# A graph attention kernel: ScalarE's exponentials ahead of its table copies, own rows transposed a block earlier

## The chip, the cores and the metric

The kernel runs on one NeuronCore of a Trainium2 chip. The metric is the device time of one execution in microseconds (us). A core has five engines with a queue of instructions each: TensorE (PE in the profile; its weight loads are PEld), VectorE (DVE), ScalarE (ACT), GpSimd (POOL) and SyncE (SP). They wait for one another through semaphores. Here GpSimd issues the gathers, SyncE issues most other DMAs.

## The reference

A graph of 6250 nodes with 256 features and 100,000 edges, sorted by destination, goes through three attention layers. The first two are of one kind (4 heads of 64), with a self loop at each node, and an ELU between them; the third has 8 heads of 32. Cut to what matters:

```python
def _gatv2_layer(x, src, dst, n, Wl, Wr, att, b):
    xl = (x @ Wl).reshape(n, H, C)
    xr = (x @ Wr).reshape(n, H, C)
    e = jax.nn.leaky_relu(xl[src] + xr[dst], NEG_SLOPE)
    logits = jnp.einsum('ehc,hc->eh', e, att)
    m = jax.ops.segment_max(logits, dst, num_segments=n)
    ex = jnp.exp(logits - m[dst])
    denom = jax.ops.segment_sum(ex, dst, num_segments=n)
    alpha = ex / (denom[dst] + 1e-16)
    msg = xl[src] * alpha[:, :, None]
    out = jax.ops.segment_sum(msg, dst, num_segments=n)
    return out.reshape(n, H * C) + b
...
h = _gatv2_layer(x, src, dst, n, Wl1, Wr1, att1, b1)
h = jax.nn.elu(h)
h = _gatv2_layer(h, src, dst, n, Wl2, Wr2, att2, b2)
...
x = _layernorm(x + _L0_gnn_ref(...), axis=-1)
x = _layernorm(x + _L1_gnn_ref(x, ...), axis=-1)
```

## The kernel before

The nodes are sorted by their number of edges and cut into 49 blocks of 128 (NB), one node to a partition. A node's neighbours lie along the columns: a block has 39 columns at first and 10 at the end, the node itself among them in the first two layers. The columns are cut into tiles `g` of at most 9 (T), for which nine buffers are kept. GpSimd fills them by one indirect DMA for each column (L1207), out of a table with a row for each node.

`layer2` runs the first two attention layers: layer 0 with `own1`, `finish1` and the table `xl1_d`, layer 1 with `own2`, `finish2` and the table `xl2_d`. The third layer follows in the last part of `tile_by_degree` and isn't touched. The text counts blocks from 0 in each layer.

There is no scheduler: each engine's instructions stand in the order in which the program calls them, and each engine takes its own in that order. So what counts is the order of calls in the loop over blocks b of `layer2`:

- `gather(b + 1)` issues the gathers of the next block. `ready(b + 1)` calls `own`, which makes the next block's own rows. In layer 0, `own1` transposes the block's features on TensorE, copies them to SBUF on ScalarE (`transposed`, L1256) and multiplies them by two matrices (`product`, L1261): `pl`, for column 0 of `g`, and `pr`, which stays in PSUM. In layer 1, `own2` takes both from a tile `two` that SyncE has loaded: a copy of `pr` to PSUM (L1516).
- `attend(b)`: on VectorE for each tile a maximum, a multiplication and a sum (L1396 to L1398) give the logits. `weights` takes their maximum over the columns (L1272), then ScalarE makes four exponentials, one for each head, with their sums (L1279), and copies the weights of the last few columns (`by`, L1286). After that `later` copies the next block's own row to column 0 (L1477 in layer 0, L1517 in layer 1). In layer 0 ScalarE also keeps the sorted positions (L1408).
- `end(b - 1)`: VectorE divides the finished sum of the block before by its denominators (L1415) and adds the bias. In layer 0 `finish1` makes the ELU: three activations on ScalarE (L1481, L1482, L1484), and on VectorE the sum of their results (L1489). In layer 1 `finish2` adds the input (L1520) and makes the layer norm: statistics on VectorE, two small activations on ScalarE (L1350, L1351), a small instruction on VectorE (L1355) and the norm on ScalarE (L1358).
- The reciprocal of the block's denominators (L1447) on VectorE.
- `weighted_sum(b)`: VectorE multiplies each tile by its weights (L1309), ScalarE does so for the last few columns, one head of one column at a time (L1308), and TensorE adds the columns up by matmuls with the identity into `acc` (L1316). After the first tile's multiplication `between` is called: it runs the function `rest` of `finish`, with L1489 or L1355. So these stand on VectorE between the first and the second multiplication.
- Then the function `last` of `finish` writes the output rows of block b - 1, which are the next layer's tables: transposes on TensorE, their copy on ScalarE (L1256), products, and copies of these (twice L1496 in layer 0; L1531 and L1532 in layer 1), and SyncE stores them.

PSUM holds two buffers each of `pr` and the weights `wt`, two of the tag "tp", which the transposes and products share, one of `acc`.

At block 47 `follow` issues the first gathers of the next layer, for its first three blocks, from rows of blocks 0 to 44 alone.

Of the kernel before, what the change touches and what calls it, by code (L numbers as in the profile page):

```python
# [26 lines left out]
F32 = mybir.dt.float32  # L27
# [8 lines left out]
P = 128  # L36
# [1092 lines left out]
def tile_by_degree(  # L1129
# [3 lines left out]
    nc = tc.nc  # L1133
# [3 lines left out]
    NB = -(-N // P)  # L1137
# [3 lines left out]
    W2 = H2 * (D2 + 1)  # L1141
# [8 lines left out]
    def per_head(t, H):  # L1150
        return t.rearrange("p (h d) -> p h d", h=H)
# [6 lines left out]
    x1 = near[:, :, CM:]  # L1158
# [43 lines left out]
    def gather_rows(b, rows, cut, own, table, of, width, j0, j1):  # L1202


        for g, (s0, s1) in zip(rows, cut):
            for j in range(max(s0 - own, j0), min(s1 - own, j1)):
                nc.gpsimd.indirect_dma_start(  # L1207
                    out=g[:, j + own - s0, :width], out_offset=None, in_=table,
                    in_offset=source(of, b, j),
                )  # L1210

    def row_tiles(b, own):
        cut = chunks(cols[b] + own)
        return [rowp.tile([P, T, RW], F32, name="g") for _ in cut], cut
# [33 lines left out]
            nc.vector.reduce_sum(bad, pb, axis=AX.X)  # L1248
            nc.vector.tensor_single_scalar(done, bad, 0.0, op=OP.is_equal)

    def transposed(work, ps, xt):
        pt = ps.tile([P, 2, P], F32, name="pt", tag="tp")
        for c in range(2):
            nc.tensor.transpose(pt[:, c, :], xt[:, c * P : (c + 1) * P], ident)
        xT = work.tile([P, 2, P], F32, name="xT")
        nc.scalar.copy(xT, pt)  # L1256
        return xT

    def product(pm, xT, w):
        for c in range(2):  # L1260
            nc.tensor.matmul(pm, xT[:, c, :], w[:, c, :], start=c == 0, stop=c == 1)  # L1261
# [6 lines left out]
    def weights(work, ps, lg, S, H, scalar=0):  # L1268


        top = work.tile([P, H], F32, name="top")
        nc.vector.tensor_reduce(  # L1272
            top, lg[:, :S, :].rearrange("p s h -> p h s"), axis=AX.X, op=OP.max, negate=True
        )
        wt = ps.tile([P, S, H], F32, name="wt")
        den = work.tile([P, H], F32, name="den")
        if H <= 4:
            for h in range(H):
                nc.scalar.activation(  # L1279
                    wt[:, :, h], lg[:, :S, h], AF.Exp, bias=top[:, h : h + 1],  # L1280
                    accum_out=den[:, h : h + 1],
                )
            by = None
            if scalar:
                by = work.tile([P, scalar, H], F32, name="by")
                nc.scalar.copy(by, wt[:, S - scalar :, :])  # L1286
            return (wt, by), lambda: den
        nc.vector.tensor_add(lg[:, :S, :], lg[:, :S, :], top[:, None, :].to_broadcast([P, S, H]))
        nc.scalar.activation(wt, lg[:, :S, :], AF.Exp)  # L1289

        def add_up():
            nc.vector.reduce_sum(den, wt.rearrange("p s h -> p h s"), axis=AX.X)
            return den

        return (wt, None), add_up
# [64 lines left out]
    def layer2(i, table, of, width, start, own, finish, follow):  # L1360

        with ExitStack() as es:
            zp = es.enter_context(tc.tile_pool(name=f"z{i}", bufs=1))
            work = es.enter_context(tc.tile_pool(name=f"work{i}", bufs=3))
            ps = es.enter_context(tc.tile_pool(name=f"ps{i}", bufs=2, space=PSUM))
            ps1 = es.enter_context(tc.tile_pool(name=f"ps1{i}", bufs=1, space=PSUM))  # L1370
            pst = es.enter_context(tc.tile_pool(name=f"pst{i}", bufs=2, space=PSUM))
            at = ps1.tile([P, W2], F32, name="at")
            nc.scalar.copy(at, att[i])
            state = {}

            def gather(b):
                first = EARLY[b] if b in begun else 0
                rows, cut = begun.pop(b) if first else row_tiles(b, 1)
                gather_rows(b, rows, cut, 1, table, of, width, first, cols[b])
                state[b] = [rows, cut]  # L1380

            later = []

            def ready(b):
                pr, put = own(work, ps, pst, b, state[b][0][0][:, 0, :W2])
                state[b].append(pr)
                later.append(put)

            def attend(b):
                rows, cut, xr = state.pop(b)  # L1390
                S = cols[b] + 1
                lg = work.tile([P, CM + 1, H2], F32, name="lg")
                for g, (s0, s1) in zip(rows, cut):
                    n = s1 - s0
                    z = zp.tile([P, T, W2], F32, name="z")[:, :n, :]
                    nc.vector.tensor_max(z, g[:, :n, :W2], xr[:, None, :].to_broadcast([P, n, W2]))  # L1396
                    nc.vector.tensor_mul(z, z, at[:, None, :].to_broadcast([P, n, W2]))  # L1397
                    nc.vector.reduce_sum(  # L1398
                        lg[:, s0:s1, :], z.rearrange("p t (h d) -> p t h d", h=H2), axis=AX.X
                    )  # L1400
                few = min(S // 3, cut[-1][1] - cut[-1][0] - 1) if b + 1 < NB else 0
                wt, new = weights(work, ps, lg, S, H2, few)
                while later:
                    later.pop()()
                if i == 0:
                    for g, (s0, s1) in zip(rows, cut):
                        s = max(s0, 1)
                        nc.scalar.copy(spots[:, b, s - 1 : s1 - 1], g[:, s - s0 : s1 - s0, W2])  # L1408
                    if 0 < b <= len(EARLY):
                        sort_sources(work, pst, b - 1)  # L1410
                return rows, cut, wt, new

            def end(b, acc, den):
                h = work.tile([P, F], F32, name="h")
                nc.vector.tensor_mul(  # L1415
                    per_head(h, H2), per_head(acc, H2),
                    den.unsqueeze(2).to_broadcast([P, H2, D2]),
                )
                if i == 0:
                    nc.vector.tensor_add(h, h, bias[0])  # L1420
                return finish(work, pst, b, h)

            for b in range(3):
                if (i, b) not in loaded:
                    start(b)
            gather(0)
            ready(0)
            later.pop()()
            if i == 0:
                none(state[0][2])  # L1430
            acc, den, rest = None, None, None
            for b in range(NB):
                if b + 3 < NB:
                    start(b + 3)
                if b + 1 < NB:
                    gather(b + 1)
                if b + 2 == NB:
                    follow()
                if b + 1 < NB:
                    ready(b + 1)  # L1440
                rows, cut, wt, new = attend(b)
                if b:
                    rest = end(b - 1, acc, den)
                if i == 0:
                    nc.vector.tensor_add(x1[:, b, :], x1[:, b, :], bias[1])
                den = new()
                nc.vector.reciprocal(den, den)  # L1447

                last = []

                def between():
                    if b:
                        last.append(rest())

                acc = weighted_sum(ps1, rows, cut, wt, H2, D2 + 1, between)
                if i == 0 and b + 1 < NB:
                    none(state[b + 1][2])
                if last:
                    last[0]()
            end(NB - 1, acc, den)()()  # L1460

    def none(t):
# [5 lines left out]
            out=near[:, b, :], out_offset=None, in_=near_d[:, :], in_offset=node(b)  # L1468
        )

    def own1(work, ps, pst, b, row):
        xT = transposed(work, pst, x1[:, b, :])
        pl = pst.tile([P, W2], F32, name="pl", tag="tp")
        product(pl, xT, wc[0][:, 0])
        pr = ps.tile([P, W2], F32, name="pr")
        product(pr, xT, wc[0][:, 1])
        return pr, lambda: nc.scalar.copy(row, pl)  # L1477

    def finish1(work, pst, b, h):
        neg = work.tile([P, F], F32, name="neg")  # L1480
# [29 lines left out]
        nc.sync.dma_start(two[:, 1, :], xr2_d[b * P : (b + 1) * P])  # L1510
        kept[b] = two

    def own2(work, ps, pst, b, row):
        two = kept.pop(b)
        pr = ps.tile([P, W2], F32, name="pr")
        nc.scalar.copy(pr, two[:, 1, :])  # L1516
        return pr, lambda: nc.scalar.copy(row, two[:, 0, :])  # L1517

    def finish2(work, pst, b, h):
        nc.vector.tensor_add(h, h, x1[:, b, :])  # L1520
# [18 lines left out]
    kept, loaded = {}, set()  # L1539
# [11 lines left out]
    with ExitStack() as es:  # L1551
        work = es.enter_context(tc.tile_pool(name="work3", bufs=3))
        ps = es.enter_context(tc.tile_pool(name="ps3", bufs=3, space=PSUM))
        state = {}
# [50 lines left out]
        acc, den, puts, rest = None, None, {}, None  # L1605
        for b in range(NB):
# [5 lines left out]
            if b:  # L1612
                rest = end(b - 1, acc, den)
# [39 lines left out]
```

## Time and profile before

| What | us |
|---|---|
| median of 3 runs | 3907.3 (3907.01 to 3914.32) |
| profiled execution | 3906.24 |
| its span, first to last instruction | 3904.4 |
| VectorE busy | 2859.7 (73%) |
| GpSimd busy | 2558.8 (66%) |
| TensorE matmuls busy | 1465.1 (38%) |
| ScalarE busy | 1093.2 (28%) |

Layer 0 lasts from about 220 to 1440 us of the span, layer 1 from about 1540 to 2720, the third layer from there to the end; what comes before 220 us sorts the nodes and builds the first table. A row of a group of instructions tells line, engine, operation, the tiles written and read with their sizes, the count, then busy time in us and the mean of one in ns, then the idle time of the engine just before them and what ended most of it. "remote" there is a releaser that the trace doesn't tell. A row of a timeline has the start and duration in us, engine, line, operation, tiles, count, and in brackets the idle time before it. A row of windows has for each engine its busy time and number of instructions, then the granted TensorE clock, the DMA share and GB/s.

### The profile page before, as it was taken

How to read it: one execution, taken by the hardware profiler on the slowest of the kernel's cores; microseconds unless marked ns; L12 is line 12 of the kernel's file. 1: busy time of each engine (PE TensorE's matmuls, PEld its weight loads, DVE VectorE, ACT ScalarE, POOL GpSimd, SP SyncE). 2: the span in 40 equal slices, each digit the busy share in tenths (PEclk: the TensorE clock that was granted, in tenths of full speed). 3: DMA queues.
4: the chain of work that ended last, by engine and by line, in shares of the span. 5: the costliest groups of instructions: out<-in, count | busy, mean ns of one | idle time of the engine just before them, and what ended most of it. 6: DMA issues, size and time to landing. Idle time of an engine off the chain costs nothing.

```text
span 3904.4 us, 23669 instructions
## 1 busy us (share of the span) xinstructions
PE 1465.1 (38%) x5147; PEld 1100.0 (28%) x5147; DVE 2859.7 (73%) x2624; ACT 1093.2 (28%) x4179; POOL 2558.8 (66%) x2642
## 2 busy tenths in 40 slices
PE   5335655646667653355545455554000000000000
PEld 4223443435455542243433334442000000000000
DVE  6267888768888867798877889895686666666655
ACT  2123433434445441243334334442000000000000
POOL 6466666666666654666666666663777777777774
PEclk8667787777888886676766777776555555555555
DMA  8443333333334333333434344342433333333332
GB/s 192 101 94 100 104 103 100 105 102 103 105 103 107 104 102 71 103 106 105 112 104 111 107 110 111 109 111 69 100 107 105 97 96 97 97 97 96 97 97 56
DMA packets 197563, 399.62 MB, mean 102 GB/s; under 512 B 63516, under 2 KB 115994, under 8 KB 197396
## 3 DMA queue, kind: packets, MB, share of 16 engines
q0 software_dynamic: 123488, 342.06, 33.7%
q1 hardware_dynamic: 66226, 54.22, 4.9%
q10 hardware_dynamic: 7698, 1.74, 0.4%
q8 instruction: 45, 0.74, 0.1%
q14 instruction: 106, 0.87, 0.1%
HBM read 357.84 MB, written 40.42 MB: 102 GB/s over the span
## 4 chain that ended last, share of the span: by engine, by line
issue 24%; POOL 21%; PE 16%; DVE 14%; another core or an unknown queue 12%; ACT 9%; DMA 2%; DVEq 0%; SPq 0%; ACTq 0%; POOLq 0%
POOL g L1207 19%; PE acc L1316 10%; ACT g L1308 4%; PE pm L1261 3%; DVE z L1397 3%; DVE z L1396 3%; DVE lg L1398 3%; ACT wt L1279 2%; DVE weighted L1327 1%; DVE g L1309 1%; DMA g<-xl_d,near_r 1%; POOL out L1597 1%; ACT xT L1256 1%; PE pl L1261 1%
## 5 line engine op out<-in xcount | busy, mean ns | idle before, releaser
L1207 POOL DMA_INDIRECT g<-xl_d,near_r x1591 | 1508.6, 948 | 843.6 <-issue 455.7
L1316 PE MATMUL acc<-g,ident 128*128 128x256 f32 x3452 | 1015.0, 455 | 910.1 <-issue 361.4
L1316 PEld LDWEIGHTS acc<-g,ident 128*128 128x128 f32 x3452 | 768.0, 229 | 1152.9 <-issue 617.4
L1207 POOL DMA_INDIRECT g<-whs_d,near_r x777 | 802.2, 1032 | 293.9 <-issue 251.9
L1308 ACT ACTIVATE g<-g,by 128x64 f32<-128x64 f32 x2064 | 550.4, 337 | 331.3 <-issue 328.0
L1396 DVE TENSOR_TENSOR z<-g,pr 128x1820 f32<-128x1820 f32 (+4 forms) x236 | 503.4, 2133 | 39.3 <-DMA g<-xl_d,near_r 25.7
L1397 DVE TENSOR_TENSOR z<-z,at 128x1820 f32<-128x1820 f32 (+4 forms) x236 | 503.7, 2134 | 8.1
L1398 DVE TENSOR_REDUCE lg<-z 128x28 f32<-128x1820 f32 (+4 forms) x236 | 503.6, 2134 | 8.1
L1336 DVE TENSOR_REDUCE acc_v<-weighted 128x256 f32<-128x4096 f32 (+16 forms) x49 | 349.2, 7127 | 11.7 <-remote 6.1
L1309 DVE TENSOR_TENSOR g<-g,wt 128x1792 f32<-128x1792 f32 (+5 forms) x236 | 353.8, 1516 | 2.9
L1567 DVE TENSOR_TENSOR lg<-g,s_r 128x56 f32<-128x56 f32 (+4 forms) x113 | 22.8, 214 | 367.4 <-DMA g<-whs_d,near_r 300.0
L1289 ACT ACTIVATE wt<-lg 128x128 f32<-128x128 f32 (+17 forms) x49 | 14.0, 285 | 901.2 <-DVE top L1272 309.9
L1256 ACT COPY xT<-pt 128x256 f32<-128x256 f32 x147 | 55.0, 374 | 704.8 <-remote 367.3
L1327 DVE TENSOR_TENSOR weighted<-g,wt 128x1792 f32<-128x1792 f32 (+4 forms) x113 | 229.5, 2048 | 0.0
L1447 DVE RECIPROCAL den<-den 128x4 f32<-128x4 f32 x98 | 17.4, 177 | 226.8 <-ACT wt L1279 158.9
L1279 ACT ACTIVATE wt<-lg,top 128x19 f32<-128x19 f32 (+14 forms) x392 | 116.1, 296 | 209.0 <-DVE top L1272 83.7
L1415 DVE TENSOR_TENSOR h<-acc,den 128x256 f32<-128x256 f32 x98 | 40.7, 416 | 166.8 <-remote 122.3
L1261 PE MATMUL pm<-wh_cat,xT 128*128 128x272 f32 x196 | 83.9, 568 | 192.7 <-issue 108.7
L1261 PE MATMUL pm<-wcat,xT 128*128 128x260 f32 x392 | 138.5, 512 | 45.8 <-ACT xT L1256 44.8
L1261 PEld LDWEIGHTS pm<-wcat,xT 128*128 128x128 f32 x392 | 96.9, 261 | 82.1 <-ACT xT L1256 61.7
L1261 PEld LDWEIGHTS pm<-wh_cat,xT 128*128 128x128 f32 x196 | 46.0, 260 | 213.5 <-issue 113.5
L1597 POOL DMA_INDIRECT out<-y,node_i x49 | 50.3, 1027 | 49.6 <-ACT y L1358 35.6
(180 smaller groups left out, 1511.1 us busy)
## 6 DMA issues: line engine op xcount, KB each, us to landing
g<-xl_d,near_r POOLq DMA_INDIRECT x1591
g<-whs_d,near_r POOLq DMA_INDIRECT x777
whs_d<-row SPq DMA_DIRECT2D x49, 132.0 KB
xl_d<-xl SPq DMA_DIRECT2D x49, 130.0 KB
xl_d<-row SPq DMA_DIRECT2D x49, 130.0 KB
xr_d<-row SPq DMA_DIRECT2D x49, 130.0 KB
two<-xl_d SPq DMA_DIRECT2D x49, 130.0 KB
two<-xr_d SPq DMA_DIRECT2D x49, 130.0 KB
```

The lines of the kernel that those rows point to most:

```text
L1207: nc.gpsimd.indirect_dma_start(out=g[:, j + own - s0, :width], out_offset=None, in_=table, in_offset=source(of, b, j),)
L1256: nc.scalar.copy(xT, pt)
L1261: nc.tensor.matmul(pm, xT[:, c, :], w[:, c, :], start=c == 0, stop=c == 1)
L1279: nc.scalar.activation(wt[:, :, h], lg[:, :S, h], AF.Exp, bias=top[:, h : h + 1], accum_out=den[:, h : h + 1],)
L1308: nc.scalar.mul(g4[:, t, h, :], g4[:, t, h, :], by[:, t - m, h : h + 1])
L1309: nc.vector.tensor_mul(g4[:, :m], g4[:, :m], wt[:, s0 : s0 + m, :].unsqueeze(3).to_broadcast([P, m, H, F // H]),)
L1316: nc.tensor.matmul(acc, ident, g4[:, t], start=s0 + t == 0, stop=s0 + t == S - 1)
L1327: nc.vector.tensor_mul(prod[:, s0 - base : s1 - base, :].rearrange("p t (h d) -> p t h d", h=H), g[:, :n, :F].rearrange("p t (h d) -> p t ...
L1336: nc.vector.reduce_sum(part, prod[:, : s1 - base, :].rearrange("p s f -> p f s"), axis=AX.X)
L1396: nc.vector.tensor_max(z, g[:, :n, :W2], xr[:, None, :].to_broadcast([P, n, W2]))
L1397: nc.vector.tensor_mul(z, z, at[:, None, :].to_broadcast([P, n, W2]))
L1398: nc.vector.reduce_sum(lg[:, s0:s1, :], z.rearrange("p t (h d) -> p t h d", h=H2), axis=AX.X)
```

## The change

In `layer2` three calls move. `own` is cut in two: its first half (the transposes and their copy, in layer 0 alone) runs two blocks ahead, after `end(b - 1)` and the reciprocal, and gives back a function for the products. `ready(b + 1)`, which calls that function and the copy to column 0, moves from ahead of `attend(b)` into it, to just after the exponentials. `last(b - 1)` moves from the end of iteration b to iteration b + 1, after its exponentials and after `ready`. In `own1` the product `pr` is made ahead of `pl`, and the transposed tile has a name, and so three buffers, of its own.

So ScalarE's order in a block of layer 0 was: table copies of block b - 2 (L1256, twice L1496), copy of the own transposes for b + 1 (L1256), exponentials of b (L1279, L1286), L1477, L1408, the ELU of b - 1 (L1481 to L1484), multiplications of b (L1308). It becomes: exponentials of b, L1477 for b + 1, table copies of b - 2, L1408, the ELU of b - 1, copy of the own transposes for b + 2, multiplications of b. In layer 1 the copies L1516 and L1517 follow the exponentials, then the table copies (L1256, L1531, L1532), then L1350, L1351, L1358 and the multiplications. TensorE's order was sum of b - 1, transposes and products of the output b - 2, own transposes and products for b + 1; it becomes sum of b - 1, own products for b + 1, transposes and products of the output b - 2, own transposes for b + 2. VectorE, GpSimd and SyncE keep their orders.

```diff
-    def transposed(work, ps, xt):
+    def transposed(work, ps, xt, name="xT"):
...
-        xT = work.tile([P, 2, P], F32, name="xT")
+        xT = work.tile([P, 2, P], F32, name=name)
...
-            later = []
+            mine, due = {}, []
 
             def ready(b):
-                pr, put = own(work, ps, pst, b, state[b][0][0][:, 0, :W2])
+                pr, put = mine.pop(b)(state[b][0][0][:, 0, :W2])
                 state[b].append(pr)
-                later.append(put)
+                put()
...
                 wt, new = weights(work, ps, lg, S, H2, few)
-                while later:
-                    later.pop()()
+                if b + 1 < NB:
+                    ready(b + 1)
+                while due:
+                    due.pop()()
...
             gather(0)
+            for b in range(2):
+                mine[b] = own(work, ps, pst, b)
             ready(0)
-            later.pop()()
...
-                if b + 1 < NB:
-                    ready(b + 1)
                 rows, cut, wt, new = attend(b)
...
-                last = []
+                if b + 2 < NB:
+                    mine[b + 2] = own(work, ps, pst, b + 2)
 
                 def between():
                     if b:
-                        last.append(rest())
+                        due.append(rest())
 
                 acc = weighted_sum(ps1, rows, cut, wt, H2, D2 + 1, between)
                 if i == 0 and b + 1 < NB:
                     none(state[b + 1][2])
-                if last:
-                    last[0]()
+            due.pop()()
             end(NB - 1, acc, den)()()
...
-    def own1(work, ps, pst, b, row):
-        xT = transposed(work, pst, x1[:, b, :])
-        pl = pst.tile([P, W2], F32, name="pl", tag="tp")
-        product(pl, xT, wc[0][:, 0])
-        pr = ps.tile([P, W2], F32, name="pr")
-        product(pr, xT, wc[0][:, 1])
-        return pr, lambda: nc.scalar.copy(row, pl)
+    def own1(work, ps, pst, b):
+        xT = transposed(work, pst, x1[:, b, :], "xo")
+
+        def products(row):
+            pr = ps.tile([P, W2], F32, name="pr")
+            product(pr, xT, wc[0][:, 1])
+            pl = pst.tile([P, W2], F32, name="pl", tag="tp")
+            product(pl, xT, wc[0][:, 0])
+            return pr, lambda: nc.scalar.copy(row, pl)
+
+        return products
...
-    def own2(work, ps, pst, b, row):
-        two = kept.pop(b)
-        pr = ps.tile([P, W2], F32, name="pr")
-        nc.scalar.copy(pr, two[:, 1, :])
-        return pr, lambda: nc.scalar.copy(row, two[:, 0, :])
+    def own2(work, ps, pst, b):
+        def products(row):
+            two = kept.pop(b)
+            pr = ps.tile([P, W2], F32, name="pr")
+            nc.scalar.copy(pr, two[:, 1, :])
+            return pr, lambda: nc.scalar.copy(row, two[:, 0, :])
+
+        return products
```

## The prediction

> **What bounds the kernel now.** I read the page first (shares of the engines, the chain), then the busy time by stage, then the groups of VectorE in each stage with the idle time before them, and last the timeline of one block of each layer. VectorE (DVE) is the busiest engine, 73%, and in the two attention layers it is at four fifths and more:
>
> ```profile
> core 0: us, PE busy (x) PEld busy (x) DVE busy (x) ACT busy (x) POOL busy (x), PEclk, DMA share, GB/s
> 220.00:1440.00 1220.00, 751.39 (x2608) 553.17 (x2608) 983.41 (x883) 509.57 (x1920) 786.15 (x828) 0.79 0.38 102
> 1600.00:2670.00 1070.00, 556.97 (x1882) 425.92 (x1882) 934.49 (x760) 436.29 (x1776) 686.34 (x725) 0.72 0.40 107
> ```
>
> The first row is layer 0 of the two (47 blocks), the second layer 1. GpSimd (POOL), which issues the gathers, has a third of each stage left. So what VectorE waits for sets the pace. In layer 0 and in layer 1 its groups with idle time before them are these:
>
> ```profile
> L1447 DVE RECIPROCAL den<-den 128x4 f32<-128x4 f32 x47 | 8.3, 178 | 132.5 <-ACT wt L1279 88.7 <-issue 43.8
> L1415 DVE TENSOR_TENSOR h<-acc,den 128x256 f32<-128x256 f32 x47 | 19.5, 415 | 61.4 <-PE acc L1316 33.6 <-remote 27.8
> ...
> L1447 DVE RECIPROCAL den<-den 128x4 f32<-128x4 f32 x47 | 8.3, 177 | 76.0 <-ACT wt L1279 64.3 <-issue 11.7
> L1415 DVE TENSOR_TENSOR h<-acc,den 128x256 f32<-128x256 f32 x46 | 19.1, 415 | 42.2 <-remote 42.2
> ```
>
> The reciprocal waits for ScalarE's exponentials. Why they are late, a block of layer 0 tells (ScalarE's rows, then VectorE's):
>
> ```profile
> 1062.35 0.37 ACT L1256 COPY xT<-pt 128x256 f32<-128x256 f32 x1 [7.69 <-PE pt L1254]
> 1064.91 0.38 ACT L1496 COPY row<-pm 128x260 f32<-128x260 f32 x1 [2.19 <-PE pm L1261]
> 1066.14 0.37 ACT L1496 COPY row<-pm 128x256 f32<-128x256 f32 x1 [0.85 <-PE pm L1261]
> 1066.41 0.38 ACT L1256 COPY xT<-pt 128x256 f32<-128x256 f32 x1
> 1066.67 0.31 ACT L1279 ACTIVATE wt<-lg,top 128x16 f32<-128x16 f32 x1
> ...
> 1068.54 0.38 ACT L1477 COPY g<-pl 128x260 f32<-128x260 f32 x1
> 1068.81 0.41 ACT L1408 CAST near_r<-g 128x7 int32<-128x7 f32 x2
> 1069.13 0.41 ACT L1481 ACTIVATE neg<-h 128x256 f32<-128x256 f32 x1
> ...
> 1069.89 0.40 ACT L1484 ACTIVATE pos<-h 128x256 f32<-128x256 f32 x1
> ...
> 1062.88 0.26 DVE L1272 TENSOR_REDUCE top<-lg 128x4 f32<-128x64 f32 x1
> ...
> 1068.47 0.18 DVE L1447 RECIPROCAL den<-den 128x4 f32<-128x4 f32 x1 [4.20 <-ACT wt L1279]
> 1068.68 2.29 DVE L1309 TENSOR_TENSOR g<-g,wt 128x2048 f32<-128x2048 f32 x1
> 1070.89 0.42 DVE L1489 SCALAR_TENSOR_TENSOR h<-neg,pos 128x256 f32<-128x256 f32 x1
> ...
> 1071.23 0.95 DVE L1309 TENSOR_TENSOR g<-g,wt 128x768 f32<-128x768 f32 x1
> ```
>
> The maximum was there at 1063.14, the exponentials began at 1066.67: 3.5 us of row copies and their waits for TensorE stood ahead of them. And see the place of L1489: between the two multiplications L1309, in order, and it reads what ScalarE's L1484 writes. Today L1484 is done before the first multiplication ends, so L1489 costs no wait.
>
> **What the Trainium skill says.** "TensorE: Matmul & The Clock Gate", section "Architectural detail": ScalarE and VectorE take their instructions in strict order. The trace agrees: no row of theirs overtakes another. Same page, "HAM oscillation": TensorE falls to half clock after idle gaps of about 3.4 us; the granted clock here is 0.79 and 0.72 in the two layers, and 0.50 in the last stage, where no matmul runs. "Perfetto Trace Analysis", section "Per-engine timelines": a matmul's end in a trace is computed, not observed. That fits the waits called remote: VectorE sat 27.8 us (twice) and 42.2 us (seven times) before L1415, though the last sum shows long ended.
>
> **The change part by part.**
>
> *Gain: exponentials first.* They now follow ScalarE's multiplications of the block before, and wait for the maximum alone. What idle time stays before the reciprocal: the four of them take 1.8 us from the maximum to the reciprocal, VectorE's own work there lasts 1.13 us in layer 0 (1063.14 to 1064.27), and 1.46 us in layer 1 (one addition and the two statistics more, 2272.73 to 2274.19). So 0.69 and 0.35 us stay. 132.5 - 47 x 0.69 = 100 us and 76.0 - 47 x 0.35 = 60 us go: 160 us in all.
>
> *Cost in layer 0: L1489 becomes a wait.* ScalarE's order after the exponentials is now: the small copy, the own row's copy L1477, then the copies for the next table (L1256, twice L1496), and only then casts and L1481 to L1484. From the end of the last exponential (1068.31 in the block above): the copy L1256 at +0.55, if its transposes are ready; the first L1496 2.17 us later (mean of the 49 blocks, 1.61 to 2.57, as it waits for two matmuls); the second 1.11 us later (0.88 to 1.73, one of 7.31 left out); the casts 0.27 later; the end of L1484 1.54 after them. Sum: 5.64 us. VectorE's L1489 is due at 1070.89, that is at +2.58. So VectorE stands for 3.06 us in every block, with the second multiplication and all the next block's work queued behind it: 47 x 3.06 = 144 us. Nothing hides this: VectorE is the pacing engine.
>
> *Cost in layer 1: L1355 becomes a wait.* It also stands between two multiplications and reads L1351. After the exponentials (end 2274.89) now come the copies L1516 and L1517, then L1256 at +0.88, L1531 2.23 later (mean; 1.64 to 2.64 and two outliers), L1532 +0.27, L1350 +0.06, the end of L1351 +0.52: 3.96 us. L1355 was at 2277.46, +2.57. That is 1.39 us, 47 times, less 10 us for the seven blocks where VectorE waits for the sum longer anyway: 55 us.
>
> *Products behind the sum.* TensorE's queue is now sum, own products, output's transposes. The own products are in the timeline as two rows of 1.15 and 1.04 us, 2.2 us together, and the output's transposes as 0.63 us. Where ScalarE's multiplications run nearly to the maximum (blocks 7 to 14 of layer 0; in block 10 from 573.08 to a last sum at 593.22), L1477 and L1256 wait for these 1 to 2.5 us more: 15 us. In other blocks these are done before the exponentials end, at no cost. The sum's start moves from +2.6 to about +5, as the next table's matmuls stand ahead of it; the sum has 20 us until L1415 asks for it, so nothing, and up to 85 us if that cover is gone (rival below).
>
> *Rows a block ahead, buffers.* Transposes of own rows are as many as before, their copy (0.38 us) leaves the way of the exponentials and stands ahead of ScalarE's multiplications: nothing. The new tile has three buffers and is used one block later. Row tiles too: nothing.
>
> *DMAs.* The two stores of a block's output rows come 7 us later on SP. Only GpSimd's first gather for layer 1 waits for one of them (1418.10, for a store issued at 1415.55), and after those early gathers GpSimd stands still for 23.9 us until 1493.93 for the last rows. 7 us lie within it. Gathers and stores are the same in number and order: nothing. The same at the end of layer 1.
>
> Sum: -160 + 144 + 55 + 15 = +54 us. The profiled execution took 3906.2 us (span 3904.4), the median is 3907.3, 1 us above. Forecast 3960 us.
>
> **Rivals.**
>
> *The waits are short and the gain stays (faster).* If TensorE is at full clock when the two copies wait, they cost 1.61 + 0.88 and 1.65 us: waits of 2.27 and 0.81 us, 107 and 38 us in all. If half of the 70 us of remote waits before L1415 goes too, the sum is -160 + 107 + 38 - 35 = -50: 3857 us. For it: the clock depends on how TensorE's idle time is cut, and that is what is changed; the short values are the commonest single ones. Against: the means hold long values for half of the blocks.
>
> *ScalarE or TensorE sets the pace (much slower).* ScalarE's multiplications begin 4 us later (after L1256 of the own rows, some 6 us behind the exponentials, not 1.9). Where they last over some 15 us, as in blocks 4 to 21 of layer 0 (14 to 27 us), they end after the next maximum, and L1415 waits for the sum. 17 blocks x up to 5 us = 85 us more: 4045 us. Against: the new wait itself gives them 3 us.
>
> *It cancels.* Gain and waits agree within the 7.8 us that count as no change: 3907 us. It needs waits of 2.4 us in layer 0 with 55 us in layer 1, between forecast and first rival.
>
> That the change doesn't do what it says is excluded: the built order has the exponentials ahead of L1256 and L1496 in all blocks.
>
> **How the numbers follow.** Forecast 0.57 (its own range 3925 to 3995), faster rival 0.22, much slower 0.15, cancelled 0.06. Both slower cases sum to 0.72; I take 0.71, and 0.23 for faster, as a short wait has room below. No change, within 0.2% (about what a measurement of this kernel can tell from none), 0.06. The range reaches into both rivals and leaves out the far half of each, about 0.1 on either side: 3875 to 4020 us.
>
> **What would show it.** Right: idle time before the reciprocal falls to about 33 us in layer 0 and 16 in layer 1; the group of L1489 (the same instruction, a few lines down) shows some 140 us of idle time put down to ScalarE's copies or L1484, that of L1355 some 55 put down to L1351; the first sums begin 5 us after the exponentials. Wrong: these waits are under 100 us together, or the idle time shows up before L1415.

## The result and the profile after

The changed kernel takes 4005.59 us (4001.76 to 4006.53, 4 runs), the kernel before 3910.81 us beside it (3907.01 to 3917.67, 4 runs): a ratio of 1.0246, 95% interval 1.0227 to 1.0266. The profiled execution has a span of 4003.3 us where the one before had 3904.4, so 99 us more. The forecast was 3960 us.

The groups of VectorE that changed, over the whole span. The first four are of the kernel after (denominators, division of the sum, ELU sum, layer norm):

```profile
L1449 DVE RECIPROCAL den<-den 128x4 f32<-128x4 f32 x98 | 17.2, 176 | 47.7 <-ACT wt L1279 29.1 <-issue 18.6
L1418 DVE TENSOR_TENSOR h<-acc,den 128x256 f32<-128x256 f32 x98 | 40.7, 415 | 176.6 <-remote 141.9 <-PE acc L1316 26.8 <-PE pl L1261 8.0
L1495 DVE SCALAR_TENSOR_TENSOR h<-neg,pos 128x256 f32<-128x256 f32 x49 | 20.9, 427 | 200.8 <-ACT pos L1490 137.5 <-issue 51.9 <-ACT g L1308 6.3
L1355 DVE SCALAR_TENSOR_TENSOR sd<-mv,sd 128x1 f32<-128x1 f32 x98 | 15.3, 157 | 91.3 <-ACT sd L1351 24.1 <-issue 21.6 <-ACT row L1540 21.5
```

and these are the same four groups in the kernel before:

```profile
L1447 DVE RECIPROCAL den<-den 128x4 f32<-128x4 f32 x98 | 17.4, 177 | 226.8 <-ACT wt L1279 158.9 <-issue 67.9
L1415 DVE TENSOR_TENSOR h<-acc,den 128x256 f32<-128x256 f32 x98 | 40.7, 416 | 166.8 <-remote 122.3 <-PE acc L1316 44.4
L1489 DVE SCALAR_TENSOR_TENSOR h<-neg,pos 128x256 f32<-128x256 f32 x49 | 20.6, 421 | 14.8 <-ACT pos L1484 12.4 <-ACT g L1308 2.1 <-issue 0.3
L1355 DVE SCALAR_TENSOR_TENSOR sd<-mv,sd 128x1 f32<-128x1 f32 x98 | 15.2, 155 | 1.8 <-ACT sd L1351 1.8
```

Busy times hardly differ; read the number behind the second bar, the idle time. Before the denominators it fell from 226.8 to 47.7 us. Before the ELU sum it rose by 186 us, before the layer norm's small instruction by 90, before the division by 10. By this account the change won 179 us and lost 285.

A block of layer 0 in the timeline after, with the engines' rows one after the other (ScalarE from the first exponential on, then TensorE, then VectorE; start and duration in us):

```profile
1087.88 0.29 ACT L1279 ACTIVATE wt<-lg,top 128x16 f32<-128x16 f32 x1 [10.81 <-issue]
...
1089.22 0.29 ACT L1279 ACTIVATE wt<-lg,top 128x16 f32<-128x16 f32 x1
...
1090.01 0.39 ACT L1256 COPY xT<-pt 128x256 f32<-128x256 f32 x1
1092.59 0.38 ACT L1502 COPY row<-pm 128x260 f32<-128x260 f32 x1 [2.19 <-issue]
1094.26 0.37 ACT L1502 COPY row<-pm 128x256 f32<-128x256 f32 x1 [1.29 <-issue]
...
1095.68 0.40 ACT L1490 ACTIVATE pos<-h 128x256 f32<-128x256 f32 x1
...
1090.45 3.77 PE L1261 MATMUL pm<-wcat,xT 128*128 128x260 f32 x8 [10.65 <-ACT xT L1256]
...
1087.58 0.26 DVE L1272 TENSOR_REDUCE top<-lg 128x4 f32<-128x64 f32 x1
...
1089.67 0.18 DVE L1449 RECIPROCAL den<-den 128x4 f32<-128x4 f32 x1 [0.70 <-ACT wt L1279]
1089.88 2.29 DVE L1309 TENSOR_TENSOR g<-g,wt 128x2048 f32<-128x2048 f32 x1
1096.12 0.43 DVE L1495 SCALAR_TENSOR_TENSOR h<-neg,pos 128x256 f32<-128x256 f32 x1 [3.93 <-ACT pos L1490]
```

The exponentials now follow the maximum at once, and VectorE waits 0.70 us for them. But `pos` comes behind two copies that wait for TensorE's products, and VectorE stands 3.93 us between its two multiplications. TensorE stood still for 10.65 us before these products, and they became slower, as the product groups show (before, then after; shortest, median and longest in ns). That the pause is the reason is tested below.

```profile
L1261 PE MATMUL pm<-wcat,xT x392: 382/426/802, 321.6 to 1491.5; 128*128 128x260 f32 x196
```

```profile
L1261 PE MATMUL pm<-wcat,xT x392: 382/641/802, 328.4 to 1568.6; 128*128 128x260 f32 x196
```

### The profile page after: what moved, and what is told of

Same layout as the page of the kernel before. It is cut to its first block, busy times and chain, and to the rows that moved or that the text cites. A ratio compares the mean times of both kernels' runs of the same rounds, so it can differ in the third digit from the quotient of the medians.

```text
span 4003.3 us, 23717 instructions
## 1 busy us (share of the span) xinstructions
PE 1396.5 (35%) x5147; PEld 1079.3 (27%) x5147; DVE 2865.5 (72%) x2624; ACT 1071.3 (27%) x4179; POOL 2556.3 (64%) x2642
## 5 line engine op out<-in xcount | busy, mean ns | idle before, releaser
L1316 PE MATMUL acc<-g,ident 128*128 128x256 f32 x3452 | 910.1, 418 | 358.4 <-issue 121.9
L1207 POOL DMA_INDIRECT g<-whs_d,near_r x777 | 803.9, 1035 | 286.9 <-issue 250.1
L1316 PEld LDWEIGHTS acc<-g,ident 128*128 128x128 f32 x3452 | 708.1, 212 | 554.3 <-issue 193.9
L1308 ACT ACTIVATE g<-g,by 128x64 f32<-128x64 f32 x2064 | 529.8, 337 | 192.4 <-issue 189.6
L1279 ACT ACTIVATE wt<-lg,top 128x19 f32<-128x19 f32 (+14 forms) x392 | 115.2, 294 | 1076.1 <-DVE top L1272 622.1
L1336 DVE TENSOR_REDUCE acc_v<-weighted 128x256 f32<-128x4096 f32 (+16 forms) x49 | 349.2, 7127 | 11.7 <-remote 4.5
L1261 PE MATMUL pm<-wcat,xT 128*128 128x260 f32 x392 | 177.6, 630 | 465.1 <-ACT xT L1256 206.7
L1261 PE MATMUL pm<-wh_cat,xT 128*128 128x272 f32 x196 | 104.9, 690 | 528.6 <-ACT xT L1256 234.7
L1261 PEld LDWEIGHTS pm<-wcat,xT 128*128 128x128 f32 x392 | 119.1, 319 | 504.3 <-ACT xT L1256 212.4
L1261 PEld LDWEIGHTS pm<-wh_cat,xT 128*128 128x128 f32 x196 | 56.6, 319 | 552.0 <-ACT xT L1256 240.4
L1495 DVE SCALAR_TENSOR_TENSOR h<-neg,pos 128x256 f32<-128x256 f32 x49 | 20.9, 427 | 200.8 <-ACT pos L1490 137.5
L1502 ACT COPY row<-pm 128x260 f32<-128x260 f32 x98 | 36.7, 374 | 166.3 <-issue 90.9
```

The lines of the kernel that those rows point to most:

```text
L1207: nc.gpsimd.indirect_dma_start(out=g[:, j + own - s0, :width], out_offset=None, in_=table, in_offset=source(of, b, j),)
L1279: nc.scalar.activation(wt[:, :, h], lg[:, :S, h], AF.Exp, bias=top[:, h : h + 1], accum_out=den[:, h : h + 1],)
L1308: nc.scalar.mul(g4[:, t, h, :], g4[:, t, h, :], by[:, t - m, h : h + 1])
L1316: nc.tensor.matmul(acc, ident, g4[:, t], start=s0 + t == 0, stop=s0 + t == S - 1)
L1336: nc.vector.reduce_sum(part, prod[:, : s1 - base, :].rearrange("p s f -> p f s"), axis=AX.X)
```

## The experiments

There are twelve runs, on three chips. On one chip, A below, the kernel before takes 3910 and 3908 us, as in the result, so A stands for the conditions of the result too, though the record doesn't name the result's chip. On the other two, B below, it takes 3409 and 3412 us. Every ratio is to the kernel before on the same chip. This difference was not looked for, and it turned out to be the best witness.

**The copies for the next table behind the ELU and the statistics, run on B and on A.** All else of the change stays, the early exponentials too:

```diff
                 if b + 1 < NB:
                     ready(b + 1)
-                while due:
-                    due.pop()()
...
                 if b:
                     rest = end(b - 1, acc, den)
+                while due:
+                    due.pop()()
```

> The copies for the next table are issued after the ELU and statistics activations of the finished block instead of ahead of them; all else of the change stays. Theory 1 (the loss is VectorE waiting for pos and sd, which stand on ScalarE behind the copies for the next table): the idle time before the ELU sum (200.8 us) and before sd (91.3 us) falls to about 15 and 25 us or less, so that up to 250 us of the 4006 come back; where ScalarE's own work then sets the pace some of that is not seen, so 3750 to 3850 us. Theory 2 (the loss is the late own-row products or the late multiplications of ScalarE, h waiting for the sum): the sum is as late as before or later, since the copies move nearer to ScalarE's multiplications; the time stays at 3960 to 4050 us and the idle time moves to h.

On B: 3417.97 us, ratio 1.0028 (1.0017 to 1.0040).

> The copies for the next table behind the ELU and statistics activations, once more, to see it where the kernel before takes 3910 us. Theory 1 (the change's gain before the denominators, 179 us, is real there, and its loss is the waits for pos and sd alone): both waits fall from 216 + 92 to under 40 us, the idle time before the denominators stays near 48 us, and the time is 3740 to 3800 us, ratio about 0.965. Theory 2 (ScalarE's loop, stretched by gaps of 0.1 us between its multiplications, sets the pace once the waits are gone): the waits go, but h waits for the sum 50 to 100 us longer; 3820 to 3900 us. Should the kernel before take 3409 us in this draw, both expect 1.003 again.

On A: 3910.18 us, ratio 1.0001 (0.9989 to 1.0014). Three groups of VectorE in the run on A:

```profile
L1416 DVE TENSOR_TENSOR h<-acc,den 128x256 f32<-128x256 f32 x98 | 41.0, 418 | 361.0 <-remote 301.1 <-PE acc L1316 42.3 <-PE pt L1254 17.4
L1495 DVE SCALAR_TENSOR_TENSOR h<-neg,pos 128x256 f32<-128x256 f32 x49 | 20.8, 425 | 34.7 <-ACT pos L1490 19.9 <-ACT neg L1487 13.8 <-ACT xT L1256 0.9
L1449 DVE RECIPROCAL den<-den 128x4 f32<-128x4 f32 x98 | 16.7, 170 | 31.4 <-ACT wt L1279 25.0 <-issue 6.3
```

and the division in the run on B:

```profile
L1416 DVE TENSOR_TENSOR h<-acc,den 128x256 f32<-128x256 f32 x98 | 40.6, 414 | 11.7 <-PE acc L1316 11.7
```

Both new waits went, and the loss with them: on both chips the time is within 3 parts in a thousand of the kernel before. But on A the gain did not come out. The idle time before the denominators stayed low, 31.4 us, and turned up before the division, 361.0 us instead of 166.8. The expectation of 3740 to 3800 us fell; the second theory had the move of the wait right but not its size (50 to 100 us expected, 194 measured), and it blamed ScalarE, of which more below.

**The copies back at the end of the iteration, run on B and on A.** Own rows a block ahead and the order of the own products stay:

```diff
                 if b + 1 < NB:
                     ready(b + 1)
-                while due:
-                    due.pop()()
...
                 if i == 0 and b + 1 < NB:
                     none(state[b + 1][2])
-            due.pop()()
+                while due:
+                    due.pop()()
```

> The copies for the next table go back to the end of the iteration, behind ScalarE's multiplications and ahead of the next exponentials; the own rows a block ahead and the order of the own products stay as changed. Theory 1 (the order of ScalarE alone makes both the gain and the loss): the idle time before the ELU sum and sd falls back to about 15 and 2 us, the idle time before the denominators returns to about 225 us, and the time is that of the kernel before within 1%, 3875 to 3945 us. Theory 2 (own rows a block ahead or the new product order carry the loss): 3980 us or more, with the idle time before den and another stall on top of it.

> The copies for the next table back at the end of the iteration, to see it where the kernel before takes 3910 us. Theory 1 (placing those copies ahead of the ELU is the whole loss, and taking them from ahead of the exponentials the whole gain): the waits for pos and sd gone, the idle time before the denominators back at about 230 us; within 1% of the kernel before, 3870 to 3950 us. Theory 2 (part of the gain came from the own rows' transposes and products, which here stay out of the way of the exponentials): the idle time before the denominators falls by half, 3780 to 3850 us.

3409.66 us on B, 1.0003 (0.9994 to 1.0012); 3908.88 us on A, 0.9995 (0.9979 to 1.0011). The idle time before the denominators is 221.1 us on A, and 52.2 us on B, where the expectation had it return to about 225. So the other parts of the change cost nothing. And the idle time that the change was to remove is there on A alone.

**Copies and stores behind ScalarE's multiplications, on B.** As in the first experiment the transposes and products for the next table stand behind the ELU and the statistics. Their copies out of PSUM and the stores move behind the weighted sum, and the own rows' transposes to right behind the previous own products (cut to the calls):

```diff
+                puts = [due.pop()() for _ in range(len(due))]
...
                 acc = weighted_sum(ps1, rows, cut, wt, H2, D2 + 1, between)
...
+                for put in puts:
+                    put()
```

> Transposes and products for the next table stand before the weighted sum as in the run above, the copies out of PSUM and the stores after ScalarE's multiplications, and the own rows' transposes directly behind the previous own products. Theory 1: with no wait of ScalarE for TensorE ahead of anything that VectorE needs, both kinds of wait stay gone and ScalarE's idle time ahead of its multiplications goes too; at or under the kernel above, about 3750 us (3700 to 3830). Theory 2 (ScalarE's total of work sets the pace once the waits are gone): no gain over the kernel above, 3800 to 3880 us.

3424.53 us, ratio 1.0049 (1.0032 to 1.0066). The copies no longer wait (7.4 us in all before those of layer 0, 168.1 in the first experiment on the same chip), yet nothing is gained. The forecasts of 3750 and 3800 us were made for a kernel before of 3910 us.

**TensorE kept busy ahead of the products, on B.**

```diff
             product(pl, xT, wc[0][:, 0])
+            for _ in range(8 if b > 21 else 0):
+                product(pr, xT, wc[0][:, 1])
```

> The changed kernel with the first own product of blocks 22 to 48 of the first layer done nine times instead of once, so that TensorE has work in the 10.7 us in which it idles ahead of the products for the next table. Theory 1 (those products last 641 ns in the median instead of 426 since TensorE's clock falls in that idle time, and this makes the wait before the ELU sum 4.1 us instead of the forecast 3.1): in those blocks the products fall to about 430 ns and the wait before the ELU sum to 3.0 to 3.3 us, 27 blocks x 0.9 = 25 us less, 3970 to 3990 us. Theory 2 (the granted clock comes from a throttle over a longer stretch, or the wait is not set by these products): products and wait stay, or get longer where the repeats are in their way, 4005 to 4040 us.

3672.32 us, ratio 1.0775 (1.0757 to 1.0793). The blocks before the repeats begin, and those with them, in two stretches of the trace (ELU sum, then products):

```profile
L1497 DVE SCALAR_TENSOR_TENSOR h<-neg,pos 128x256 f32<-128x256 f32 x20 | 8.5, 425 | 80.5 <-ACT pos L1492 80.5
L1261 PE MATMUL pm<-wcat,xT 128*128 128x260 f32 x164 | 78.1, 656 | 250.0 <-ACT xT L1256 250.0
...
L1497 DVE SCALAR_TENSOR_TENSOR h<-neg,pos 128x256 f32<-128x256 f32 x27 | 11.5, 426 | 85.7 <-ACT pos L1492 85.7
L1261 PE MATMUL pm<-wcat,xT 128*128 128x260 f32 x224 | 77.5, 506 | 77.7 <-ACT xT L1256 77.7
```

The wait fell from 4.03 us a block to 3.17, and a product from 656 to 506 ns. These are different blocks; the same 27 without repeats, in the changed kernel with half of its sums below (on the other chip of B), have 110.8 us of wait and 629 ns. So 25 us went, as expected. Where the products were fast throughout (396 ns in the mean), a block waited 2.4 to 2.6 us; where TensorE had again paused for 3.6 us ahead of them, up to 4.1. In the blocks with repeats, pauses of up to 2.1 us left the products at 395 or 396 ns, pauses of 2.8 to 2.9 us gave 395 to 620, and those from 3.5 us on 487 to 661 (means of a block's eight). That a longer pause makes them slower, and slower products the wait longer, is shown. It is not the whole wait.

**Both kernels unchanged, on A.**

> The kernel before, unchanged, for a profile beside those of the experiments, in which it took 3409 us where the profile shown first had 3907. Theory 1 (the extra 500 us of the first profile are stalls that the profile files under issue and remote, outside the order of the instructions): busy times as in the first profile within 3%, and the idle time before the denominators, h and ScalarE's multiplications far under its 226.8, 166.8 and 331 us. Theory 2 (the work itself was slower then): busy times of VectorE and ScalarE 10% lower now, the idle shares alike.

> The changed kernel, unchanged, in the conditions of the four experiments. Theory 1 (the waits of VectorE for pos and sd, 170 + 95 us in the run with the repeated products, come from the order of ScalarE's queue and stay, while the 179 us that the change took from before the denominators are mostly absent here): about 3660 us, ratio 1.065 to 1.08. Theory 2 (gain and loss shrink alike): ratio as in the result, 1.02 to 1.03, 3480 to 3510 us; the rest of the 3672 us of the run with repeats is then due to the repeats.

3920.59 us for the kernel before in one run, and 4007.49 us for the changed one, ratio 1.0245 (1.0222 to 1.0268), the result again. Both expectations were made for a kernel before of 3409 us, so on this chip neither could be decided.

The new profile of the kernel before shows what holds VectorE up on A. A block of layer 1, TensorE first, then GpSimd and ScalarE:

```profile
1877.79 0.36 PEld L1254 LDWEIGHTS pt<-ident,near_r 128*128 128x128 f32 x2
1878.00 0.38 PE L1254 MATMUL pt<-ident,near_r 128*128 128x128 f32 x2
...
1883.12 0.95 POOL L1207 DMA_INDIRECT g<-xl_d,near_r  x1 [0.30 <-issue]
1887.57 0.94 POOL L1207 DMA_INDIRECT g<-xl_d,near_r  x1 [3.50 <-remote]
1887.67 0.37 ACT L1256 COPY xT<-pt 128x256 f32<-128x256 f32 x1 [13.62 <-remote]
```

By the trace TensorE had finished the transposes `pt` at 1878.38. ScalarE's copy, which reads them and has nothing else to wait for, starts at 1887.67; and GpSimd's gather into a tile that TensorE's sums had read starts within 0.1 us of it, after a pause. Two engines that wait for TensorE are let go together, 9 us after its recorded end. So the releaser that the trace calls remote is TensorE, late. The trace also holds the times at which each engine counted up its semaphore, though the views don't print them, and they show it. TensorE's semaphore is the only one that this copy waits for. It has entries at 1878.10, 1883.00, 1886.50 and 1887.22 us, and then ten more, each 0.04 us after the last, to 1887.65. Almost all of them stand for one column of the sum, two matmuls, and these pairs lie 0.43 us apart in the trace. Work at that pace cannot end every 0.04 us, so most of it was done before its signals came. Over this run 725 of 1842 entries follow the one ahead within 0.06 us. With the copies at the end on B none of 2210 does, and half of them come within 0.014 us of the recorded end of a matmul. No run on A was without this lateness.

Behind this copy stand the products and the exponentials, and so it looked as if the order of ScalarE's queue were the limit. In blocks 12 to 15 of layer 1 (61 to 64 over both layers; from one reciprocal to the next, by the timelines) the period is 27.14, 25.72, 25.74 and 25.59 us in this run, 27.06, 25.71, 25.71 and 25.68 with the copies at the end, 27.10, 25.74, 25.69 and 25.68 with the copies behind the statistics: the same, whatever ScalarE's order. On B the latter has 24.29, 24.28, 23.46 and 23.20 us, and VectorE pauses for 0.4 us in each.

These four blocks are not the rule. In layer 0 single blocks on A do get shorter with the early exponentials, down to the 21.1 us of B, but others pay for it: one waits 18.18 us before the division. What stays the same is the sum. From the first reciprocal to the last, layer 0 takes 1265, 1268 and 1269 us in these three orders on A, and layer 1 takes 1174, 1169 and 1159. On B, with the copies at the end and with those behind the statistics, they take 1046 and 1013 us.

**Own products behind those for the next table, on A.**

```diff
-                if b + 1 < NB:
-                    ready(b + 1)
                 while due:
                     due.pop()()
+                if b + 1 < NB:
+                    ready(b + 1)
```

> The changed kernel with the products for the next table ahead of the next block's own products, as before the change. Theory 1 (ScalarE's copies in front of pos and sd make the waits, whatever the order of the products): waits before the ELU sum and sd as in the changed kernel beside it, within 30 us in sum, the time within 1% of it. Theory 2 (the own products stand in the way of the products for the next table): the waits lose over 1 us a block, 50 us or more in all.

4101.26 us, ratio 1.0497 (1.0472 to 1.0521), 94 us over the changed kernel beside it. The ELU sum:

```profile
L1495 DVE SCALAR_TENSOR_TENSOR h<-neg,pos 128x256 f32<-128x256 f32 x49 | 20.8, 425 | 340.4 <-ACT pos L1490 311.3 <-issue 19.3 <-ACT neg L1487 9.8
```

and in the changed kernel beside it:

```profile
L1495 DVE SCALAR_TENSOR_TENSOR h<-neg,pos 128x256 f32<-128x256 f32 x49 | 20.9, 426 | 216.4 <-ACT pos L1490 125.4 <-issue 76.7 <-ACT neg L1487 14.3
```

So 124 us more. Neither theory had this: the own row's copy too stands ahead of `pos`, and with this order it waits until TensorE has done the products for the table and then the own ones (140.9 us of idle time before that copy, 39.8 in the changed kernel). Each product that ScalarE awaits ahead of `pos` adds to VectorE's wait.

**With every second sum left out, on B.** These kernels leave out about half of the rows, to see whether TensorE's sums bound the kernel.

```diff
-            for t in range(n):
+            for t in [t for t in range(n) if (s0 + t) % 2 == 0 or s0 + t == S - 1]:
                 nc.tensor.matmul(acc, ident, g4[:, t], start=s0 + t == 0, stop=s0 + t == S - 1)
```

> The kernel before with every second of TensorE's sums over the gathered rows left out (about 860 of 1726 sums; all else is issued as before, so the output lacks half of the rows). Theory 1 (in the conditions of the result TensorE's signals set the block's period, 27.1 and 25.7 us in blocks 60 and 63 whatever ScalarE's order, and the idle time before the denominators is the room that they leave): with half of the sums the period falls to VectorE's own, 24.3 and 23.5 us; 3909 falls to 3450 to 3600 us, and most of the 227 us before the denominators go without any change of order. Theory 2 (ScalarE's late exponentials set it, as the prediction had it): the idle time before the denominators stays above 150 us and the time above 3750 us. Where the kernel before takes 3409 us, both expect no change.

> The changed kernel with every second of TensorE's sums left out in the same way. Theory 1 (the waits before the ELU sum and sd cost 265 us, of which TensorE's period hides 170 in the result): the waits stay at 200 us or more in sum, and the run is 200 to 280 us above half_before, where the result had 97 between them. Theory 2 (gain and loss are those of the accounts of idle time): 60 to 130 us above half_before.

> The changed kernel with the copies for the next table behind the ELU and statistics activations, with every second of TensorE's sums left out. Theory 1: within 30 us of half_before, the wait of h for the sum (361 us with all sums) under 80 us. Theory 2 (earlier exponentials are worth their 180 us wherever TensorE is not late): 120 us or more below half_before.

3410.20 us for the kernel before with half of the sums, 0.9993 (0.9985 to 1.0002); 3703.30 us for the changed one, 1.0855 (1.0836 to 1.0873); 3423.08 us with the copies behind the ELU, 1.0033 (1.0020 to 1.0045). TensorE's sums do not bound the kernel on B, as was expected for such a chip. For the second kernel the first theory was nearer (200 to 280 us over the first, 293 measured), for the third it held (within 30 us, 13 measured); what the sums do to the time on A this doesn't show. Denominators, ELU sum and layer norm in the first of them, then in the second:

```profile
L1447 DVE RECIPROCAL den<-den 128x4 f32<-128x4 f32 x98 | 17.4, 177 | 52.1 <-ACT wt L1279 52.1
L1489 DVE SCALAR_TENSOR_TENSOR h<-neg,pos 128x256 f32<-128x256 f32 x49 | 20.6, 421 | 3.7 <-ACT pos L1484 3.7
L1355 DVE SCALAR_TENSOR_TENSOR sd<-mv,sd 128x1 f32<-128x1 f32 x98 | 15.1, 154 | 1.8 <-ACT sd L1351 1.8
```

```profile
L1449 DVE RECIPROCAL den<-den 128x4 f32<-128x4 f32 x98 | 17.4, 177 | 52.0 <-ACT wt L1279 52.0
L1495 DVE SCALAR_TENSOR_TENSOR h<-neg,pos 128x256 f32<-128x256 f32 x49 | 20.8, 425 | 194.9 <-ACT pos L1490 194.9
L1355 DVE SCALAR_TENSOR_TENSOR sd<-mv,sd 128x1 f32<-128x1 f32 x98 | 15.3, 156 | 95.5 <-ACT sd L1351 95.5
```

This is the account without anything in its way. The denominators gain 0.1 us, the two waits cost 191 + 94 = 285 us, and the time differs by 293; 8 us are not accounted for. The changed kernel with all of its sums wasn't run on B; the run with the repeated products, which has its order, lies 263 us over the kernel before there.

No version was faster than the kernel before. On B VectorE pauses there for 0.7 and 0.4 us a block ahead of the reciprocal in the two layers, so earlier exponentials have nothing left to give.

## Why the prediction was right on the side and short on the size

- *Gain, 160 us.* The idle time went as worked out: in layer 0 from 132.5 to 28.4 us, in layer 1 from 76.0 to 15.6. That this is time saved is the step that failed. The prediction said "what VectorE waits for sets the pace" and took ScalarE's queue for the cause; with the early exponentials and without the new waits the kernel takes 3910 us on A, as before, with the idle time before the division. Each layer takes about the same time there in three orders, and the wait before the division ends with TensorE's late signals. On B there was nothing to gain: 52 us of idle time before the denominators in every order that ran there. The prediction had seen the "remote" waits, 70 us before the division, but not that the copy L1256, which releases the rest, waits for the same cause.
- *Cost in layer 0, 144 us.* The mechanism is right, and with that of layer 1 it makes the whole loss: with the copies behind the ELU and the statistics it is gone. The size was short: 191 us on B, 186 in the result. In the block above the first copy comes 2.58 us after L1256 and the second 1.67 later, where the sum took 2.17 and 1.11 from the kernel before; together 0.97 us more, and the wait there is 3.93 us instead of 3.06. Means over blocks in which part of the products were fast don't hold once the change makes TensorE idle ahead of nearly every one. "TensorE: Matmul & The Clock Gate", section "HAM oscillation" of the Trainium skill, which the prediction cites, describes such a loop: after each idle gap of more than about 3.4 us the next matmuls start at the low clock. Here the gap is 10.65 us in the block shown, and the median product takes 641 ns against a shortest of 382.
- *Cost in layer 1, 55 us.* Right in kind, 94 us on B and 90 in the result, 1.9 us a block for 1.39. The products there, too, became slower (568 to 690 ns in the mean), though no run tests this for layer 1. Of the 10 us taken off for longer waits the result shows at most 4, the difference from B.
- *Products behind the sum, 15 us.* No run has this price by itself. As a price of this order against the other it is wrong in sign: with the output's products first, and the own row's copy behind those for the table, the kernel is 94 us slower.
- *Rows a block ahead, buffers, DMAs, nothing.* Right: the run that keeps only these and the order of the own products is within 0.2% on A and B.
- *The sum, +54 us.* Measured +95 by the medians. On A the new waits, 276 us, fill the room that TensorE leaves VectorE anyway, 179 us before the denominators: 97 are left. This is an account and not an experiment; for it, blocks 12 to 15 of layer 1 take 26.65, 26.66, 25.83 and 25.59 us in the result, and 26.66, 26.65, 25.83 and 25.56 in the changed kernel with half of its sums on B. There its own waits set the period on both. The -160 stands in the sum for that room, so the total came near by luck: on B, with half of the sums, the same change costs 293 us.
- *Rivals.* The faster one needed short products, and the change itself prevents them. Of the second, the wait before the division rose by only 10 us in the result. It rose by 194 us on A in the kernel with the copies behind the ELU, but the same order on B has 11.7 us, so ScalarE's later multiplications are not its cause.

What stays open is why TensorE's signals are late on A. The recorded end of a matmul doesn't show the lateness, since it is computed ("Perfetto Trace Analysis", section "Per-engine timelines", of the Trainium skill); here such an end lies 9 us ahead of the copy that waits for it. The bursts of signals 0.04 us apart show that the signals are late even where the work is done; whether some of the work is late as well they don't tell. Halving the sums on A would show whether the amount of it counts; it wasn't tried there. Nor is A's slowness TensorE's alone: ScalarE pauses too (below), and the third layer, which has no matmuls, takes 1194 us there after the last reciprocal of layer 1 and 1084 on B.

## What to carry to other kernels

When a copy that waits for TensorE is moved ahead of something that VectorE needs in the middle of its own work, price that wait with the slow products if the move also leaves TensorE idle in front of it. Before idle time counts as gain, ask whether the pace is set elsewhere: if several engines are let go at the same moment, or if another order gives the same time, the idle time may only move. And a stall that hides another one makes a change look cheaper than it is: the same order costs 2.5% on A, and 7.8 to 8.6% on B in the two variants run there.

## What the runs showed of the hardware that was not expected

Chips differ. The same kernel takes 3908 to 3910 us on one and 3409 to 3412 on two others, from the same program. The granted clock is 0.668 on A and 0.693 on B (medians over runs of the kernel before), 4% apart, where the times are 15% apart. Whether it is the chip itself or a state that it was in isn't shown. A gather of the third layer takes GpSimd 1035 ns on A and 949 on B, those of the first two layers 948 on both. ScalarE's multiplications on A, then on B, in the kernel with the copies behind the ELU:

```profile
L1308 ACT ACTIVATE g<-g,by 128x64 f32<-128x64 f32 x2064 | 521.0, 339 | 125.0 <-issue 124.8
```

```profile
L1308 ACT ACTIVATE g<-g,by 128x64 f32<-128x64 f32 x2064 | 502.9, 339 | 0.0
```

They last the same, but on A 125 us of pauses stand between them in which nothing that the profile shows is awaited (335.3 us in the kernel before). Multiplications that follow such a pause start mostly 0.7, 1.4 or 2.1 us after the one ahead, multiples of about 0.7 us. The gaps between TensorE's late signals in the block above, 4.90, 3.50 and 0.72 us, are multiples of the same step, so the two may be one effect. On B there is no such pause. Why isn't known. The recording of the profile may have a part in it: on A the trace has 1168 entries of VectorE's semaphore for 2475 instructions that count it up, on B 2477. No run decides that.
